# Where in a block of 256 TensorE's instructions are aligned: place 0 or place 60

## The chip, the core and the metric

One Trainium2 chip, one core of it. The metric is the device time of one execution in microseconds (us). The kernel is one launch, and its whole instruction stream is written out: no loop on the chip.

## The reference, cut to what matters

```python
# layer 0: a recurrence over T = 256 steps, N = 64 rows, D = 1024
xW = einsum('ntd,dh->nth', x, Wx) + b          # x: (64, 256, 1024) f32
h  = cond                                       # (64, 1024)
for t in range(256):
    h = tanh(h @ Wh + xW[:, t]);  h_t[:, t] = h
x = x + h_t
# layer 1: an orthonormal Haar transform, a gate, and its inverse; the gate is
# constant over the transform, so it is  x + x * gate
gate = sigmoid(silu(cond @ W1.T + b1) @ W2.T + b2)
x = x + x * gate[:, None, :]
```

So each of 256 steps needs a 64 x 1024 by 1024 x 1024 product with the step before it, and beside that all of x is multiplied by Wx once.

## The kernel before, in words

**Pairs.** The 256 steps are taken two at a time, in 128 pairs. Pair i has a slab of x (128 partitions x 1024) that holds both steps. Its product with Wx is made on full 128-row tiles; the product with h of each step is made with Strassen's scheme on 32-column strips of the array.

**The x product of a pair** (`XWork.whole`, L334 to L347) is 48 matmuls of 128x512, written by `x_matmul` at L277: x and Wx are split into high and low parts, and the parts are multiplied as 16 matmuls into `mixed` (x2), then 16 into `main` (x1), then 16 into `main` (x0). Below, "x matmul 0 to 47" counts them in that order. Each is a weight load (LDWEIGHTS) and a matmul, thus two instructions.

**The h product of a step** is seven calls of `strassen_product` (L193, matmuls at L198), each 16 matmuls in four strips. In f32 every one of those becomes two weight loads and two matmuls, so one call is 32 matmul records and 64 instructions. A pair of steps has 14 calls: "product 1 to 14" below.

**The order of TensorE's work** is written by hand: `manual_schedule` fixes it to the order of the program. In the first stage (t below ALONE = 12) the x product is interleaved with single steps. From t = 12 the loop at L746 runs groups of two steps (`groups`, L635, M = 2, the last group has four steps), and at the end of each group `beside_x` (L657) writes the next pair's x product, stores the sums of the pair before it to DRAM and loads them back in another layout (`store`, `reload`), and has VectorE, ScalarE and GpSimd finish, scale and store. So TensorE's stream is: 48 x matmuls, 14 h products, 48 x matmuls, and so on.

**The alignment.** `whole(True)` puts the directive `nc.tensor.addr_align(BLOCK)` (L346) before x matmul 46, the last but one of a pair. `BLOCK` is 256. The directive has no work of its own: when the program is loaded it is replaced by as many NOP instructions as it takes until the next instruction stands at a multiple of 256 in TensorE's stream. `beside_x` asks for it in every call that writes one pair alone (`not many`, L669); in this kernel that is 121 times, the first before t = 12. Nothing in the first stage is aligned.

Between the h products stand a few EVENT_SEMAPHORE instructions, which TensorE's sequencer handles alone: five in each pair, ahead of products 2, 8, 12 and 14 and ahead of x matmul 16.

With 96 instructions of x matmuls, 896 of h products and 5 waits, a pair has 997 instructions; 27 NOPs make it 1024, four blocks of 256. So from the second alignment on, each alignment takes 27 NOPs, and the four borders between blocks lie at the same four instructions in every pair. The border at which a new block begins is called an edge below; edge 0 is the one in the x product, edges 1, 2 and 3 lie in the h products.

Of the kernel before, what the change touches and what calls it, by code (L numbers as in the profile page):

```python
# [80 lines left out]
ALONE = LATE + B + 1  # L81
RINGS = 1024
BLOCK = 256


@with_exitstack
def tile_cond_resid(
# [14 lines left out]
    nc = tc.nc  # L102
# [172 lines left out]
    def x_matmul(acc, v, which: int, h: int, k: int, start=False, stop=False) -> None:  # L275

        nc.tensor.matmul(  # L277
            out=acc[h],
            lhsT=v[:, k * P : (k + 1) * P],
            rhs=wx_s[k][which][:, h * HALF : (h + 1) * HALF],  # L280
            start=start and k == 0,
            stop=stop and k == B - 1,
        )

    class XWork:
# [48 lines left out]
        def whole(self, aligned: bool = False) -> None:  # L334

            self.begin()
            for h in range(2):
                for k in range(B):
                    x_matmul(self.mixed, self.x2, 2, h, k, True, True)
            for h in range(2):  # L340
                for k in range(B):
                    x_matmul(self.main, self.x1, 1, h, k, start=True)
            for h in range(2):
                for k in range(B):
                    if aligned and h == 1 and k == B - 2:
                        nc.tensor.addr_align(BLOCK)  # L346
                    x_matmul(self.main, self.x0, 0, h, k, stop=True)  # L347

        def first(self) -> None:
# [519 lines left out]
```

## Time and profile before

| | us |
|---|---|
| median of 3 runs (lowest, highest) | 3055.76 (3055.02, 3056.12) |
| the profiled execution | 3057.8 |
| its span, first to last instruction | 3056.0 |
| TensorE busy, of the span | 3036.1 (99%) |
| VectorE, ScalarE, GpSimd busy | 1796.7, 871.0, 844.9 |
| start of one pair's x product to the next, usual | 23.47 |
| the same for the first aligned pair | 35.18 |

The page gives busy time by engine (PE is TensorE's matmuls, PEld its weight loads), then the chain that ended last, then groups of instructions by source line. A busy share of 99% says that one engine is the bound, not that every stretch is tight; for this change the stretches in which it is not busy are what has to be found, and the chain in order of time lists them as pieces named "issue". The view of one source line shows the NOPs: they stand at L346, on TensorE's sequencer (PEldq). Instruction fetches appear among the DMA queues as q8 and q14, kind "instruction".

### The profile page before, as it was taken

The numbers are of one execution on the slowest core, as the hardware profiler recorded it, in microseconds if no ns is written. First come the engines' busy times: TensorE is split into PE (matmuls) and PEld (weight loads), VectorE is DVE, ScalarE is ACT, GpSimd is POOL, SyncE is SP. The second block draws the span as 40 slices with busy tenths as digits, with TensorE's granted clock in tenths as the row PEclk, the third lists the DMA queues.
The fourth block names the chain that finished last, engine by engine and source line by source line (L and its number), as shares of the span: only waits on it lengthen the run. The fifth ranks groups of instructions, "written<-read, shape, count | busy, mean of one in ns | idle before, by whom it ended". The sixth has DMA issues, their size and how long they took to land.

```text
span 3056.0 us, 144905 instructions
## 1 busy us (share of the span) xinstructions
PE 3036.1 (99%) x63862; PEld 2709.2 (89%) x63862; DVE 1796.7 (59%) x4928; ACT 871.0 (29%) x2641; POOL 844.9 (28%) x521
## 2 busy tenths in 40 slices
PE   9989999999999999999999999999999999999999
PEld 6879988998899889988988899889888988898888
DVE  8555555555555555555555555555555555555555
ACT  3223222322232223222322232222222222222222
POOL 2222333323222322232223222322232223222321
PEclk9999999999999999999999999999999999999999
DMA  7323333233222322232223222322222222222222
GB/s 263 122 86 99 98 114 104 94 102 99 93 85 92 100 91 85 93 101 90 86 92 101 90 85 93 101 90 86 94 98 91 86 95 98 91 86 96 102 85 75
DMA packets 164616, 300.59 MB, mean 98 GB/s; under 512 B 44192, under 2 KB 110496, under 8 KB 164000
## 3 DMA queue, kind: packets, MB, share of 16 engines
q1 hardware_dynamic: 163856, 290.81, 28.2%
q8 instruction: 514, 8.42, 1.2%
q14 instruction: 102, 0.84, 0.1%
q10 hardware_dynamic: 144, 0.52, 0.0%
HBM read 154.93 MB, written 136.31 MB: 95 GB/s over the span
## 4 chain that ended last, share of the span: by engine, by line
PE 99%; issue 0%; POOL 0%; DVE 0%; ACT 0%; DVEq 0%
PE main L277 30%; PE acc L198 22%; PE mixed L277 16%; PE m_h L198 15%; PE main_h L198 14%; PE m L198 1%; PE acc L215 1%; PE gate_ps L215 0%; POOL sum L323 0%; PE acc_raw L215 0%; PE unused L437 0%; DVE x L301 0%; ACT sum L322 0%; DVEq L859 0%; ACT h L759 0%
## 5 line engine op out<-in xcount | busy, mean ns | idle before, releaser
L277 PE MATMUL main<-wx,x 128*128 128x512 f32 x4064 | 946.5, 389 | 10.6 <-issue 10.1
L504 POOL TENSOR_TENSOR x<-x,factor 128x512 f32<-128x512 f32 x242 | 358.5, 1482 | 2043.7 <-issue 1177.7
L277 PEld LDWEIGHTS main<-wx,x 128*128 128x128 f32 x4064 | 762.1, 188 | 171.8 <-issue 13.1
L277 PE MATMUL mixed<-wx,x 128*128 128x512 f32 x2032 | 499.1, 397 | 0.0
L323 POOL TENSOR_TENSOR sum<-sum,b_row 128x512 f32<-128x512 f32 x254 | 448.4, 1785 | 49.9 <-ACT sum L322 43.2
L277 PEld LDWEIGHTS mixed<-wx,x 128*128 128x128 f32 x2032 | 371.6, 188 | 97.9 <-issue 24.8
L759 ACT ACTIVATE h<-h 128x128 f32<-128x128 f32 x976 | 275.7, 306 | 548.4 <-DVE h L783 331.9
L763 DVE STREAM_TRANSPOSE hT<-h 128x128 f32<-128x128 f32 x972 | 297.7, 306 | 38.3 <-ACT h L759 38.2
L301 DVE TENSOR_TENSOR x<-x,x_high 128x1024 fp32r<-128x1024 f32 x127 | 170.6, 1343 | 254.1 <-PE main L277 254.0
L379 DVE SCALAR_TENSOR_TENSOR sum<-main,sum 128x512 f32<-128x512 f32 x254 | 175.6, 691 | 217.5 <-PE main L277 215.8
L777 ACT COPY y<-m_h 128x128 f32<-128x128 f32 x244 | 65.0, 267 | 740.4 <-PE m_h L198 725.3
L198 PE MATMUL acc<-wh,s 128*32 128x128 f32 x8160 | 273.3, 273 | 0.7 <-issue 0.7
L198 PE MATMUL acc<-t,hT 128*32 128x128 f32 x8160 | 270.9, 273 | 1.6 <-issue 1.6
L198 PE MATMUL acc<-wh,hT 128*32 128x128 f32 x8160 | 270.3, 273 | 0.6 <-issue 0.6
L198 PE MATMUL m_h<-wh,hT 128*32 128x128 f32 x7808 | 262.1, 275 | 0.0
L198 PE MATMUL m_h<-t,s 128*32 128x128 f32 x7808 | 261.6, 273 | 0.0
L198 PE MATMUL main_h<-wh,s 128*32 128x128 f32 x7808 | 261.4, 273 | 0.0
L198 PE MATMUL main_h<-t,s 128*32 128x128 f32 x7808 | 258.4, 273 | 0.0
L198 PEld LDWEIGHTS m_h<-wh,hT 128*32 128x32 f32 x7808 | 209.3, 110 | 43.1 <-issue 42.9
L322 ACT ACTIVATE sum<-mixed 128x512 f32<-128x512 f32 x254 | 152.0, 599 | 321.2 <-PE mixed L277 223.0
L306 DVE SCALAR_TENSOR_TENSOR x<-x_high,x 128x1024 fp32r<-128x1024 f32 x127 | 191.3, 1506 | 87.6 <-PE mixed L277 87.5
L617 ACT COPY acc<-xw 128x128 f32<-128x128 f32 x732 | 177.9, 264 | 214.7 <-DMA xw<-sum_d 145.3
(81 smaller groups left out, 2937.3 us busy)
## 6 DMA issues: line engine op xcount, KB each, us to landing
x<-xT SPq DMA_DIRECT2D x127, 512.0 KB, 5.2
sum_d<-sum SPq DMA_DIRECT2D x127, 512.0 KB, 3.4
xw<-sum_d SPq DMA_DIRECT2D x1016, 64.0 KB, 2.1
yT<-x SPq DMA_DIRECT2D x122, 512.0 KB, 2.7
wh<-wh SPq DMA_DIRECT2D x8, 512.0 KB, 11.0
w<-w1T SPq DMA_DIRECT2D x8, 512.0 KB, 8.7
w<-w2T SPq DMA_DIRECT2D x8, 512.0 KB, 4.6
wx<-wx SPq DMA_DIRECT2D x7, 512.0 KB, 8.5
```

The source lines that it names most:

```text
L198: nc.tensor.matmul(out=out[q * R : (q + 1) * R], lhsT=a[:, k * R : (k + 1) * R], rhs=wh_s.sides[i][k][:, q], start=first and k == 0, stop= ...
L277: nc.tensor.matmul(out=acc[h], lhsT=v[:, k * P : (k + 1) * P], rhs=wx_s[k][which][:, h * HALF : (h + 1) * HALF], start=start and k == 0, s ...
L301: nc.vector.tensor_sub(self.x1, x, self.high)
L306: nc.vector.scalar_tensor_tensor(out=self.x2, in0=self.high, scalar=1.0 + DOWN, in1=pairs[i], op0=ALU.mult, op1=ALU.subtract)
L322: nc.scalar.activation(s, self.mixed[h], AF.Copy, scale=-1.0)
L323: nc.gpsimd.tensor_add(s, s, b_row[:, h * HALF : (h + 1) * HALF])
L379: nc.vector.scalar_tensor_tensor(out=v, in0=self.main[h], scalar=1.0 + DOWN, in1=v, op0=ALU.mult, op1=ALU.add)
L504: nc.gpsimd.tensor_mul(of_step(x, s), of_step(x, s), blocks(factor))
L617: nc.scalar.copy(part, xws[t // S][t % S][:, j])
L759: nc.scalar.activation(quad(h, j), quad(h, j), AF.Tanh)
L763: nc.vector.transpose(quad(hT, j), quad(h, j))
L777: nc.scalar.copy(y[:, 0], m16)
```

## The change

The directive gets an offset: the next instruction shall stand at place 60 behind a multiple of 256, instead of at the multiple. Nothing else differs; the order of all other instructions on every engine is the same.

```diff
 RINGS = 1024
 BLOCK = 256
+PLACE = 60
...
                 for k in range(B):
                     if aligned and h == 1 and k == B - 2:
-                        nc.tensor.addr_align(BLOCK)
+                        nc.tensor.addr_align(BLOCK, PLACE)
                     x_matmul(self.main, self.x0, 0, h, k, stop=True)
```

## The prediction

> **What bounds the kernel now.** I read the page first: busy time by engine, then the chain that ended last.
>
> ```profile
> PE 3036.1 (99%) x63862; PEld 2709.2 (89%) x63862; DVE 1796.7 (59%) x4928; ACT 871.0 (29%) x2641; POOL 844.9 (28%) x521
> ...
> q8 instruction: 514, 8.42, 1.2%
> ```
>
> TensorE is the bound; no other engine is near it. The directive neither adds nor removes work of an engine, so the question is only where TensorE stands still. The q8 line matters too: 514 packets of together 8.42 MB are 16.4 KB each, and TensorE's records (matmuls, weight loads, NOPs, semaphore waits) are 131,792, or 256 for each packet. So q8 brings TensorE's stream, one block at a time.
>
> Next the chain in order of time, for a stretch around the first alignment. Columns: start, length, what.
>
> ```profile
> 181.69 3.89 PE mixed L277 x16
> 185.58 6.80 PE main L277 x30
> 192.38 10.11 issue
> 202.49 1.19 PE main L277 x2
> 203.68 1.83 PE m_h L198 x32
> ...
> 216.87 3.86 PE mixed L277 x16
> ...
> 240.34 3.85 PE mixed L277 x16
> ```
>
> Before the last two x matmuls of this pair TensorE waits 10.11 us for nothing but its own instructions. This pair takes 216.87 - 181.69 = 35.18 us, the next 240.34 - 216.87 = 23.47. The excess is 11.71 us. It is the longest "issue" piece of the whole chain. Then the view of line L346, for this stretch and for the next alignment:
>
> ```profile
> L346 PEldq NOP  x197: 13/13/13, 188.2 to 202.4; - x197
> ...
> L346 PEldq NOP  x27: 13/13/13, 223.3 to 225.2; - x27
> ```
>
> The stall is padding: 197 NOPs from 188.2 to 202.4, or 14.2 / 196 = 72 ns each, though each is recorded as 13 ns. At 188.2 TensorE was at x matmul 28 while its sequencer was already ahead of x matmul 46, a lead of 17 matmuls at 0.227 us, some 4 us. 14.3 us of NOPs less that lead is the 10.1 us of idle. All later alignments have 27 NOPs, 1.9 us, which the same lead hides: those pairs run at 23.47 us. Last the windows around the stall (granted clock is the column PEclk):
>
> ```profile
> 185.40:192.40 7.00, 6.98 (x31) 5.44 (x29) 4.74 (x5) 0.60 (x1) 6.27 (x3) 1.00 0.18 75
> 192.40:202.40 10.00, 0.00 (x0) 0.00 (x0) 0.00 (x0) 0.00 (x0) 0.00 (x0) 0.64 0.00 0
> 202.40:205.30 2.90, 2.81 (x34) 2.08 (x38) 0.69 (x1) 0.00 (x0) 0.00 (x0) 0.50 0.02 6
> 205.30:216.80 11.50, 11.50 (x425) 11.29 (x414) 6.48 (x26) 4.45 (x15) 1.28 (x1) 1.00 0.06 20
> ```
>
> No engine works in those 10 us, no transfer runs, and after them TensorE has half its clock for 2.9 us: half of that, about 1.45 us, is lost. 10.11 + 1.45 is the excess, to 0.15.
>
> **What the Trainium skill says.** "TensorE: Matmul & The Clock Gate", Part 1, has the array fall to half clock after an idle window of about 3.4 us and come back after about as much work; the trace agrees (0.50 for 2.9 us after 10.1 us idle). "Runtime: NRT & Kernel Launch", Instruction fetch mechanics, has 16 KiB blocks of 256 instructions, the next one fetched while the present one runs, and calls a crossing mostly hidden; the q8 packets agree in size, "mostly" is looked at below. "PSUM — Partial Sum Buffer", Engine vs sequencer instructions, puts NOPs and semaphore instructions on the sequencer alone: so a NOP costs array time only when the lead is used up, as seen. No page gives a NOP's price; the trace's 72 ns is used.
>
> **The change part by part.**
>
> *First alignment.* 197 NOPs brought the next instruction to a multiple of 256, so unpadded it would stand at place 256 - 197 = 59. The stream ahead of it is unchanged. To reach place 60 it takes 1 NOP: 196 NOPs go, and the one left costs 0.07 us beside a lead of 4 us, nothing. With the idle goes the half clock: -10.11 - 1.45, or by the pair's length 35.18 - 23.47, -11.7 us. What is late next? VectorE, ScalarE and GpSimd had nothing to do in the 10 us, so they were waiting for x matmul 46 and did not catch up on anything; GpSimd's last piece before it ends by 191.7, the last transfer by 191. After it the order is that of every later pair, which runs at 23.47 with the same work. So I take 0 for a new wait.
>
> *The other 120 alignments.* Still 27 NOPs each: the distance between alignments is a multiple of 256 as before, and the NOPs stay where they are, ahead of x matmul 46. 0.
>
> *The edges.* All four edges of a pair move 60 places ahead. Edge 0 goes from x matmul 46 to the matmul of x matmul 29 (60 = 27 NOPs + 33). Edges 1, 2, 3 lay in the last quarter of products 4, 8 and 12; counting places, they go to the last matmul of products 3, 7 and 11. An edge costs when the next block isn't there. In the trace's fetch records each fetch begins some 0.75 to 1.8 us after the sequencer passes an edge and takes 1.1 us. Pairs lose time where the block for edge 3 lands later than about 20.04 us after the pair's start, while TensorE comes to that edge at 21.4, so a block is usable some 1.4 us after it lands. The three add up to 3.3 to 4.3 us; between edges in the h products TensorE has 128 records at 27.3 ns, 3.5 us, plus the sequencer's lead. Edge 1's block was asked for long before, so it is never late; edges 2 and 3 follow in a chain. The pair periods show what that costs: of the last 118 full pairs 98 take 23.47, 20 take 0.08 to 0.40 more, 2.9 us together, always at edge 3. Where no x product gives a rest, in the last group of four steps, every edge from the third on waits:
>
> ```profile
> 3037.95 0.41 issue
> ...
> 3045.87 0.61 issue
> ...
> 3050.18 0.70 issue
> ```
>
> There the product times grow by 0.30, 0.64, 0.25, 0.90 and about 0.99 us at five edges, 3.1 us.
>
> After the change the three h edges are still 3.5 us apart, and what covers a late block is the sequencer's lead. At the new places it can be read: the wait ahead of product 12 is handled at 1505.7, and product 12 begins at 1506.30:
>
> ```profile
> L198 PEldq EVENT_SEMAPHORE  x1: 51/51/51, 1505.7 to 1505.7; - x1
> ```
>
> and in the timeline of TensorE
>
> ```profile
> 1506.30 1.13 PE L198 MATMUL m_h<-t,s 128*32 128x128 f32 x30
> ```
>
> 0.64 us, and the same ahead of products 2, 8 and 14. The new edges 2 and 3 stand just before such a wait (51 ns), so a late block and the wait add up; against that, the last matmul of a product is needed later than one in the middle of its last quarter, by up to 0.11 us. Bounds: all 20 stalls gone, -2.9; deadline 0.1 us earlier, 27 pairs instead of 17 to 20 (counted from the landing times of edge 3's block), +1.5. I take 0. Fetches from edges 1 to 3 still fall where the DMA engines are nearly idle (from 9 to 22 us after a pair's start). The fetch from edge 0 moves from 9.4 us into the loads at about 4 us, but its block isn't used before 13 us. The last group keeps its five late edges, 60 places earlier: 0, bounds -1 and +1.
>
> *Sum.* Profiled: 3057.8 - 11.7 = 3046.1 (span 3056.0 to 3044.3). Against the median, 2.04 us less: 3055.8 - 11.7 = 3044.1. If a NOP costs less without the profiler, the stall in the median is smaller; but the profiled run is only 2.04 us longer, so at least 11.7 - 2.0 = 9.7 us is there to be saved: up to 3046.1.
>
> **The rivals.**
>
> *Late blocks in every pair (slower).* Mechanism: at the new edges 2 and 3, with a semaphore wait directly behind, the lead no longer covers the fetch. Edge 3's block lands at 19.72 us in the median. If the limit of 20.04 came 0.4 us earlier, 77 pairs of 118 would be late, by 0.2 on average plus the 0.15 a stall costs now: 27 us, less 2.9 paid already, less 11.7: +12, 3068. It decides against the gain from a limit 0.3 us earlier (55 pairs at 0.29 = 16 us). For it: the tail's 0.25 to 0.99 us. Against it: lead and spacing at the new places are measured, and differ by 0.1.
>
> *Edges fall better (faster still).* The 20 stalls vanish: 3044.1 - 2.9 = 3041.2. For it: a little more slack at a product's end; against: the chain of two fetches is the same.
>
> *No gain.* The stall is a wait for something else that the NOPs only cover, or the padding isn't what the counts say: 3055.8. Against it: 197 records one after the other fill the idle time, and all engines and queues rest.
>
> **How the numbers follow.** Forecast 0.80, at 3044.1 (its own range 3042 to 3047); edges better 0.08; late blocks 0.07; no gain 0.05. Range 3041.0 to 3048.0: the first two cases, with the bounds of the NOP's price and of the edges. About 0.2% (6 us) is what a measurement of this kernel can tell from no change. Faster by more: 0.88; within: 0.05; slower by more: 0.07.
>
> **What would show it.** Line L347 of the new kernel has 1 NOP at about 188.2 and 27 in each of 120 later pairs; the chain has no issue piece of 10 us, the clock stays at 1.00 there, and the first aligned pair takes 23.5 us. Usual pairs stay at 23.47, with 8 to 30 longer ones, the excess now at products 11 to 12. Wrong if the first pair stays over 24 us, or if the excess over 23.47 in the later pairs sums to over 6 us.

## The result

| | before | after |
|---|---|---|
| median of 6 runs each, us | 3055.95 | 3043.95 |
| lowest, highest | 3055.02, 3056.54 | 3043.23, 3046.17 |
| the profiled execution | 3057.8 | 3044.8 |
| its span | 3056.0 | 3043.0 |

The ratio is 0.9962, with a 95% interval of 0.9949 to 0.9974: the change makes the kernel faster, by 12.0 us between the medians, where 11.7 was forecast. The slowest run after is still 8.9 us under the fastest before.

### The profile page after: what moved, and what is told of

It reads as the page before. It is cut to its first block, busy times and chain, and to the rows that moved or that the text cites. A ratio compares the mean times of both kernels' runs of the same rounds, so it can differ in the third digit from the quotient of the medians.

```text
span 3043.0 us, 144709 instructions
## 1 busy us (share of the span) xinstructions
PE 3033.8 (100%) x63862; PEld 2706.8 (89%) x63862; DVE 1797.0 (59%) x4928; ACT 871.0 (29%) x2641; POOL 844.4 (28%) x521
## 4 chain that ended last, share of the span: by engine, by line
PE 98%; DMA 1%; POOL 0%; issue 0%; DVE 0%; SPq 0%; DVEq 0%; ACT 0%
PE main L278 30%; PE acc L199 22%; PE mixed L278 16%; PE m_h L199 15%; PE main_h L199 14%; PE m L199 1%; DMA h0T<-condT 0%; DMA wh<-wh 0%; DMA w<-w1T 0%; POOL sum L324 0%; PE gate_ps L216 0%; DMA x<-xT 0%; DMA b_row<-b 0%; DVE x L302 0%; SPq L134 0%
```

## The profile after

The page, engine line:

```profile
PE 3033.8 (100%) x63862; PEld 2706.8 (89%) x63862; DVE 1797.0 (59%) x4928; ACT 871.0 (29%) x2641; POOL 844.4 (28%) x521
```

The counts are those of before. TensorE is busy for 2.3 us less, and its share is up; by estimate 1.4 us of the 2.3 is half of the 2.9 us that it worked at half clock after the stall. The chain in order of time, at the first aligned pair (start, length, what; all lines are one further down in the new file):

```profile
181.15 3.89 PE mixed L278 x16
185.05 7.25 PE main L278 x32
...
204.66 3.85 PE mixed L278 x16
208.51 7.25 PE main L278 x32
```

The 32 matmuls into `main` are one piece now; before they were 30, then 10.11 us of issue, then 2. The pair takes 204.66 - 181.15 = 23.51 us instead of 35.18. The NOPs of this and of the next alignment, in the view of the directive's line:

```profile
L347 PEldq NOP  x1: 13/13/13, 187.6 to 187.6; - x1
...
L347 PEldq NOP  x27: 13/13/13, 211.1 to 213.0; - x27
```

And the windows over the same stretch (columns as in the prediction; the clock is the third number from the end):

```profile
185.00:192.00 7.00, 7.00 (x33) 5.71 (x31) 4.61 (x4) 0.60 (x1) 6.13 (x3) 1.00 0.18 75
192.00:202.00 10.00, 10.00 (x362) 9.77 (x364) 5.45 (x19) 3.79 (x12) 0.76 (x1) 1.00 0.01 3
202.00:204.60 2.60, 2.60 (x101) 2.40 (x89) 1.74 (x8) 0.68 (x3) 0.53 (x1) 1.00 0.21 83
```

TensorE is busy in all of the 10 us in which it stood still, and the clock stays at 1.00.

Where the 13.0 us between the two spans come from, by the times of the matmuls (23.467 us is the median pair; the last group is counted to the end of its last matmul):

| stretch | before | after | difference |
|---|---|---|---|
| start to the first aligned pair | 181.62 | 181.08 | -0.53 |
| first aligned pair | 35.18 | 23.51 | -11.67 |
| what the next 119 pairs take over 23.467 us each | 3.08 | 1.68 | -1.40 |
| x product and products of the last group | 38.85 | 39.10 | +0.25 |
| from TensorE's last matmul to the end | 4.71 | 5.08 | +0.37 |

The first stage has the same instructions in both kernels, so its 0.53 us is what one execution differs from another: over the ten profiles of this case that stretch ends at 180.6 to 182.4 us. The 119 pairs have 11 stalls (pairs longer by more than 0.05 us) instead of 20, at the place where edge 3 now is. One such pair in the chain:

```profile
879.25 0.87 PE m_h L199 x32
880.13 1.75 PE acc L199 x64
881.88 1.03 PE main_h L199 x32
882.90 0.91 PE m_h L199 x32
883.81 0.87 PE main_h L199 x32
```

The lines are products 8, 9 with 10, 11, 12 and 13: the delay begins at the end of product 11. In the last group late blocks still show:

```profile
3016.26 1.18 issue
...
3025.10 0.29 issue
...
3032.84 0.32 issue
```

## The experiments

The theory: the whole gain is the first padding, 197 NOPs that outlasted the sequencer's lead. The rival: the gain, or part of it, is where the edges lie in the 120 later pairs. All kernels are the changed kernel with the edit shown.

### Nearly the same edges, 255 NOPs at first

```diff
-PLACE = 60
+PLACE = 58
```

> Place 58 in all alignments instead of 60: the first alignment now has to go from place 59 once round to 58, 255 NOPs in place of 1; the edges of all later pairs move by only two places. Theory (the time lies in the first padding): 255 NOPs at 72.7 ns are 18.5 us, less a lead of 4.2 us: 14.3 us of idle and 1.45 us of half clock, so 3044 + 15.8 = 3059.8 us, slower than before the change. Rival (the gain is where the edges of the 120 later pairs lie): 3044 within 2 us.

Measured: 3060.75 us (20 runs), ratio to the kernel before 1.0017 (1.0010 to 1.0024). Two places of difference cost 16.8 us against the changed kernel's 3043.95. The chain, and the view of the directive's line:

```profile
184.59 6.80 PE main L278 x30
191.38 14.52 issue
205.91 1.19 PE main L278 x2
```

```profile
L347 PEldq NOP  x255: 13/13/13, 187.2 to 205.8; - x128
```

In this profile the first aligned pair is 16.47 us over 23.467, and the later pairs lose 1.42 us together, no more than in the changed kernel. The rival falls as the main cause. The 16.8 us between the medians agree with the 16.47 of the one profile, so the price of the NOPs is not a peculiarity of one execution. But the record gives a span and a clock for every one of these runs, so it does not show what a NOP costs in a run of which nothing is recorded.

### The edges of before without the first padding

```diff
-PLACE = 60
+PLACES = [60 + 14 * n for n in range(14)] + [0] * 200
...
-                        nc.tensor.addr_align(BLOCK, PLACE)
+                        nc.tensor.addr_align(BLOCK, PLACES.pop(0))
```

> The first alignment at place 60 (1 NOP), then 14 places further in each pair (41 NOPs, about 3 us, under the lead of 4 us) until place 0, where all later alignments stay: the edges of before without the first padding. Theory: no idle, the edges of before in some 106 pairs, so 3044 + 1.3 = 3045.3 us (20 stalls instead of 11). Rival (the edges are what pays): 3055 us or more.

Measured: 3045.12 us (5 runs), ratio 0.9967 (0.9955 to 0.9980). The theory holds: with the edges of before in some 106 pairs, but without the first padding, the gain is there. The first aligned pair takes 23.51 us; 41 NOPs in one pair cost nothing. That the number was met so closely is luck, for the loss lies elsewhere than expected, and the profiled execution, at 3047.79 us the slowest of the five, is no typical one. At edge 3 of the final place only 7 pairs stall, each by 0.08 to 0.42 us, where the kernel before had 20. Most is lost on the way: two pairs of the ramp take 0.97 and 1.34 us more, and the first pair at the final place, the last with 41 NOPs, 0.68 us. The chain in the first of the three, and SyncE's transfers in the same stretch:

```profile
384.95 0.87 PE m_h L199 x32
385.82 0.21 PE main_h L199 x7
386.04 0.70 issue
386.74 0.92 PE main_h L199 x25
```

```profile
380.49 0.55 SPq L740 DMA_DIRECT2D again<-kept  x1
381.13 0.61 SPq L634 DMA_DIRECT2D yT<-x  x1
```

Here edge 1 lies in product 2 and edge 2 in product 6, where TensorE waits. The fetch that follows edge 1 comes just behind a load of 256 KB and a store of 512 KB. By the trace's packets it begins 14.28 us after the pair's start. As the edges move ahead by 14 places from pair to pair, the same fetch had begun at 12.98 two pairs earlier and at 12.51 one pair earlier. All three late pairs have that load and then that store, at 8.3 to 11 us after their start; the pairs just before and after each have no such load and their store at 5.5 to 6.5 us, and none of them stalls. Pairs with the same transfers two pairs earlier (the one with 12.98) and between the second and the third late pair do not stall either, so the transfers alone are not enough. That the transfers hold the fetch up is argued from this order, not tried by itself.

### Paddings of eleven sizes in one kernel

```diff
-PLACE = 60
+NOPS = (40, 50, 55, 60, 65, 70, 80, 100, 130, 160, 200)
+PLACES = [60] * 10
+for nops in NOPS:
+    PLACES += [(PLACES[-1] + nops - 27) % BLOCK] * 10
+PLACES += PLACES[-1:] * 20
...
-                        nc.tensor.addr_align(BLOCK, PLACE)
+                        nc.tensor.addr_align(BLOCK, PLACES.pop(0))
```

> Place 60 at first, and every tenth alignment takes a larger padding: 40, 50, 55, 60, 65, 70, 80, 100, 130, 160 and 200 NOPs, and the edges stay ten pairs at each place that results. Theory: idle of 72.7 ns times NOPs less 4.2 us, so none up to 55, then 0.2, 0.5, 0.9, 1.6, 3.1, 5.2, 7.4, 10.3 us, and half clock only after the idles from 100 or 130 NOPs on (1.45 us each): about +34 us in all. Rival (padding is hidden, or the stall before was a wait for other work): no idle at these pairs. Beside that the places show whether any of them costs more than 0.2 us a pair.

Measured: 3081.79 us (one run, so the table compares pairs within one execution), 38 us over the changed kernel. The idle is x matmul 46's start less that of 45, less the usual 0.227 us; the excess is the pair's length over 23.467:

| NOPs | first to last NOP, us | idle | excess of the pair |
|---|---|---|---|
| 40, 50 | 2.90, 3.65 | 0.00 | 0.00 |
| 55 | 4.01 | 0.02 | 0.11 |
| 60 | 4.36 | 0.37 | 0.46 |
| 65 | 4.66 | 0.67 | 0.75 |
| 70 | 5.04 | 1.05 | 1.14 |
| 80 | 5.93 | 1.94 | 2.03 |
| 100 | 7.28 | 3.30 | 5.05 |
| 130 | 9.38 | 5.39 | 7.72 |
| 160 | 11.85 | 7.86 | 10.54 |
| 200 | 14.72 | 10.73 | 12.28 |

Up to 50 NOPs nothing; from 55 on each NOP is paid, (10.73 - 0.37) / 140 = 74 ns apiece; so the lead is 60 x 0.074 - 0.37 = 4.1 us. From 100 on the excess is 1.5 to 2.7 us more than the idle. The windows behind the padding of 100 show why (columns as before):

```profile
2074.00:2078.60 4.60, 1.63 (x26) 1.29 (x30) 0.69 (x1) 0.00 (x0) 0.00 (x0) 0.91 0.00 0
2078.60:2081.00 2.40, 2.40 (x52) 2.37 (x48) 0.00 (x0) 1.21 (x2) 0.00 (x0) 0.50 0.02 7
2081.00:2085.40 4.40, 4.40 (x164) 4.40 (x160) 1.92 (x8) 1.31 (x6) 0.00 (x0) 0.98 0.01 4
```

After 3.30 us of idle the clock is at 0.50 for 3.4 us of work; after 1.94 us it isn't. By the clock's records 3.41, 4.75, 5.49 and 3.17 us of work fall under half clock behind the four long paddings, and half of each is 1.71, 2.37, 2.74 and 1.59 us; what the pairs take beyond their idle is 1.75, 2.32, 2.68 and 1.55. So the loss is half of the work that meets the half clock, and it does not grow with the idle. The expectation had each idle right to 0.5 us but their sum 2.1 us too small, and took 1.45 us for each half clock, what the kernel before paid, so at most 5.8 us where 8.3 were lost. Together that is about the 4 us by which the total was missed. The edges stood at twelve places in this kernel; beside the paddings four pairs stall, by 0.57 us together, so none of these places is a costly one.

### No alignment at all, twice

```diff
-                    if aligned and h == 1 and k == B - 2:
-                        nc.tensor.addr_align(BLOCK, PLACE)
```

> No alignment at all: no NOPs, and the edges wander by 997 places from pair to pair, so that about half of the pairs have four edges in the h products instead of three. Theory: the first stall is gone as well, but a fourth edge costs some 0.5 us as in the last group (0.64 us at its fourth edge): 0.52 x 120 x 0.5 = 31 us, so about 3075 us (3060 to 3085). Rival (edges are hidden wherever they lie, and only padding costs): 3044 us.

Measured: 3043.18 us (4 runs), ratio 0.9962 (0.9948 to 0.9976). The expected 3075 us missed by over 30 us. The engine line of the page:

```profile
PE 3033.4 (100%) x63862; PEld 2707.3 (89%) x63862; DVE 1795.5 (59%) x4928; ACT 870.2 (29%) x2641; POOL 844.0 (28%) x521
```

The later pairs lose 2.57 us together, 13 stalls at many different products: a fourth edge costs nearly nothing. The 0.5 us given to it was taken from the last group, where no x product follows every two steps; with an x product in each pair that price doesn't carry over. Why it doesn't is not shown; that the x product lets the sequencer get ahead again is the likely reason. The same kernel once more, beside the changed kernel:

> No alignment at all, once more beside the changed kernel. Theory (only NOPs beyond the lead cost; edges cost about 2 us in all wherever they lie): 3043 to 3045 us, the same as the changed kernel within 1.5 us, and the later pairs lose 1 to 3 us together. Rival (the changed place keeps blocks from being late, and the first run without alignment was a lucky one): 3047 us or more.

> The changed kernel itself once more, as the yardstick for the three others of this series: 3044 us.

Measured: 3043.71 us without alignment (ratio 0.9960, 0.9948 to 0.9973), 3042.82 us for the changed kernel (0.9960, 0.9947 to 0.9972). The later pairs lose 3.05 us without alignment and 1.25 with it. If the alignments earn something here, it is some 1 to 2 us in a profile, and the times can't tell it from nothing.

### The place of before, the padding branched over

```diff
-                        nc.tensor.addr_align(BLOCK, PLACE)
+                        nc.tensor.addr_align(BLOCK, 0, max_nops=30)
```

> The place of before (0 behind the multiple) in all alignments, but with at most 30 NOPs executed: the first padding of 197 places becomes a branch over them, the later ones stay 27 NOPs. Theory (the executed NOPs cost, not the places): no idle at the first alignment, 3044 to 3046 us. Rival (the padding costs as such, because the block that holds it has to be fetched and left): part or all of the 10 us stays, 3050 to 3056 us.

Measured: 3042.90 us, ratio 0.9958 (0.9945 to 0.9970). The view of the directive's line at the first alignment, and the chain there:

```profile
L347 PEldq COMPARE_BRANCH  x1: 298/298/298, 187.9 to 187.9; - x1
```

```profile
181.41 3.89 PE mixed L278 x16
185.30 7.25 PE main L278 x32
192.55 1.01 PE m_h L199 x32
```

The alignment is that of before, and the next one takes 27 NOPs again, but one branch of 0.30 us replaces the execution of the 197, and the lead hides it. So it is executing them that cost, not having them. The later pairs have the edges of before, and lose 0.62 us together, with 6 stalls: fewer than the changed kernel in either of its profiles.

### Edges 40 places further ahead

```diff
-PLACE = 60
+PLACE = 100
```

> Place 100 instead of 60: 41 NOPs at the first alignment, about 3 us and so under the lead of 4 us, and all edges 40 places ahead of those of the changed kernel. Theory: 3044 us within 1.5 us. Rival (60 is the right place for the edges): slower than the changed kernel by over 2 us.

Measured: 3042.32 us, ratio 0.9956 (0.9942 to 0.9969). The first alignment:

```profile
L347 PEldq NOP  x41: 13/13/13, 188.4 to 191.3; - x41
```

No idle follows, and one of the 119 later pairs is late, by 0.29 us. Place 60 is nothing special. This is the lowest median of all, but its runs (3041.70 to 3043.59) overlap with those of the changed kernel beside it (3042.58 to 3046.15), so it is not shown to be better.

## Why the prediction was right

*The first alignment.* Forecast: 1 NOP in place of 197, -11.7 us, and nothing that takes the place of the wait. Measured: 1 NOP at 187.6, and the pair shorter by 11.67, at 23.51 us. The three runs that change the first padding alone or nearly so (255 NOPs, a branch, a ramp) move the time as this term says.

*The NOP's price in other runs than the profiled one.* The forecast kept 2 us for the case that it is lower there. The 255 NOPs show no sign of that: 16.8 us between medians, 16.5 in the profile, where the runs of one kernel spread over 3 to 4 us. A run of which nothing is recorded isn't among them.

*The half clock.* Forecast 1.45 us of the 11.7, and right for this stall, because it was read from the work that met the half clock (2.9 us, halved). It is not a price of a stall: other stalls paid 1.55 to 2.7 us, as 3.2 to 5.5 us of work fell under it.

*The other alignments.* 27 NOPs each, hidden: so it is, and the paddings of 40 and 50 show that the cover would have lasted for nearly twice as many.

*The edges.* Forecast 0, between -2.9 and +1.5, with 8 to 30 stalls at products 11 to 12. The profile shows 11 stalls there and -1.40 us. The forecast's mechanism, a block that lands too late, shows in the trace: the block for edge 3 lands 18.9 us after the pair's start in the median, and 10 of the 17 pairs where it lands at 19.20 us or later stall, but one of the 101 others (counted from the third aligned pair on). The landing in the median and the limit (19.7 and 20.0 us before) both come 0.8 us earlier, so the margin stayed about what it was. The -1.40 us can't be put down to the place: with the edges of before, the ramp kernel had 7 stalls at that edge and the branch kernel 6, 0.62 us in all. The profile of before also had slower fetches: its packets on q8 took 1.14 us in the median, those of the nine other profiles 0.96 to 1.04. In the branch kernel the block for edge 3 lands at 19.5 us in the median, 0.2 us before that of the kernel before at the same place. Why that one execution had slower fetches stays open. The fetch behind edge 0 begins 2.5 us after the pair's start, not at about 4; its block isn't needed so early, and no stall follows.

*The last group.* Forecast: its five late edges stay, 0 within 1 us. After the change its products grow by 1.48, 0.36, 0.51, 0.23 and 0.62 us, 3.2 against 3.1 before. The late ones are at the second to the sixth edge now, not the third to the seventh, so these are not the same five; that the sum came out the same is in part luck, for the changed kernel's other profile has four late edges there.

*The sum.* Profiled 3044.8 against 3046.1. The 1.3 us between them have the size of the stalls of the later pairs (-1.40); the other three small differences of the table (-0.53, +0.25, +0.37) nearly cancel. Median 3043.95 against 3044.1: a match to 0.15 us is luck, as the runs of one kernel spread over 1.5 to 2.9 us.

*The rivals.* Late blocks in every pair: 1.68 us over all 119 in place of the 27 it needed. No gain: refuted by the measured gain, and its mechanism by the 255 NOPs and the branch. Edges that fall better: no place that was kept for the whole kernel differs from the others by more than the runs do.

## What to carry to other kernels

Padding that a directive puts into TensorE's stream was executed here: count it at each place, above all at the first, where the stream ahead isn't a round number of blocks. It was free as long as the sequencer's lead lasted (here 4.1 us ahead of 128x512 matmuls, so 50 NOPs), and beyond that it was paid NOP by NOP, with the half clock on top where the idle reached 3.30 us (at 1.94 us it did not). A cap that turns long padding into a branch, or a place just after where the stream stands anyway, removed it; and before an alignment is tuned, a run without it shows what it earns: here nothing that the times can show.

## What the runs showed of the hardware that was not expected

- A NOP on TensorE's sequencer takes 74 ns of its time though it is recorded with 13; a branch over 196 places took 0.30 us.
- Idle of 1.94 us left the clock alone, idle of 3.30 us halved it. In the clock's records the stretches at half clock last 3.41, 6.83, 10.24 and 10.24 us for idles of 3.30, 5.39, 7.86 and 10.73 us, and 13.65 us for the 14.69 us behind the 255 NOPs: whole multiples of 3.41. They begin 2.9 to 4.6 us after TensorE falls idle, so how much of them falls on work varies.
- Edges that wander through all places of a pair cost 2.6 and 3.1 us in 119 pairs, hardly more than edges held in place (1.2 to 1.7 us at place 60).
